# A two-layer graph network in float32 on one core: v's bias moves from a product ahead of the loop into the eviction of the attention output, and the hand-written order of all engines is laid anew

## The chip, the core and the metric

The kernel runs on one core of a Trainium2 chip. The core has five engines with queues of their own: TensorE (PE in the profile; its weight loads are PEld), VectorE (DVE), ScalarE (ACT), GpSimd (POOL) and SyncE (SP), which here only starts transfers. An engine takes its instructions in the order of its queue and waits on semaphores where it needs another engine's result. The metric is the device time of one launch in microseconds. All arithmetic is float32.

## The reference, cut to what matters

128 graphs of 128 nodes with 512 features share one adjacency matrix. Layer 0 is masked attention with eight heads of 64, layer 1 a graph attention whose edge weights come from two row products. Both have a residual and a normalisation.

```python
q = (x @ Wq + bq).reshape(b, n, H, HD)      # k and v likewise
scores = einsum('bqhd,bkhd->bhqk', q, k) / sqrt(HD) + (1 - adj) * -1e9
attn = softmax(scores)
out = einsum('bhqk,bkhd->bqhd', attn, v).reshape(b, n, d) @ Wo + bo
x = layernorm(x + out)
h = x @ W
e = leaky_relu(s1[:, :, None] + s2[:, None, :]) * adj     # s1 = h @ a1, s2 = h @ a2
x = layernorm(x + elu(softmax(e) @ h + beta * h))
```

The rows of `attn` sum to one. A constant bv added to v therefore comes out of the attention as the same constant, and can be added to the attention output in place of v, or, as bv @ Wo, to bo.

## The kernel before

**Tiles and groups.** Two graphs make a group, so there are 64 groups (`NG`), g = 0 to 63; b0 and b1 are the graphs of a group. Five matrix products a group (q, k, v, the output projection w, and h of layer 1) are computed in Strassen-Winograd form: seven block products instead of eight, numbered 1 to 7. `product(name, g, n)` issues one: four matmuls of 128x128 for q and k, two of 128x256 for v, w and h (the profile has two records for each float32 matmul, so eight and four a product). Products 1, 3, 5 and 6 go into the first half of a one-bank PSUM tile, `main[name, g][:, 0]`, product 2 into the second half, `main[..., 1]`, and 7 and 4 into a side tile (`region`). After each of them an engine takes the half out: `take_part` on ScalarE for q, k (two ACTIVATEs that add bq or bk, L347), v and h (a copy, L341), on VectorE for w (L344); `add_block` on VectorE adds a further block to what was taken (L357). The blocks' sums and differences that the right operands need are made by `block_sum` on GpSimd (L252), those of the weights once ahead of the loop by `weight_sum` (L215 to L221).

**One graph through the kernel.** q and k give `scores` (L371), then `mask` and `row_max` (VectorE), `exps` in four pieces of two heads (ScalarE, L393), `row_inv`, `normalise` in four pieces (ScalarE, L407), a write to DRAM and a read back that turn the blocks (`attn_write`, `attn_read`), `turn_attn` (VectorE), `attend` (TensorE, L446: the attention's product with v, into a PSUM tile of 128x512), and `attend_evict`, one ScalarE copy of 128x512 (L455) to `oT`. Product w follows, with the residual that `residual` (GpSimd, L427) made of x and bo. Then come the statistics, the row products, the edge weights (again through DRAM: `weights_write`, `weights_read`, `weights_turn`), `aggregate` (TensorE, L643: the edge weights times the normalised rows), `aggregate_evict` (ScalarE copy of 128x512, L650) to `zT`, product h, ELU (`elu_exp`, `elu_max`, `elu_sum`), `norm_f` (ScalarE, 128x512, L673) and `store`.

**bv before.** `bias_product` (L463) multiplies bv, spread over 128 rows, with Wo, four matmuls of 128x512 into the tile `bop`; `bias_add` (L469) adds it to the spread bo on VectorE. Both run once, ahead of the first residuals.

**The order.** No scheduler sets the order. Each step has a place, a number: `rows(g)` lists the steps of one group, a group is `STEP` = 36.678 further than the one ahead of it, `last_rows(g)` lists the last two groups, `other` holds the places of groups 0 to 3 and NG-4, NG-3, and `at(...)` those of one-time steps. All are sorted by place and issued in that order (L1088), so the places of one engine's steps are its queue. A place of -21 is a step that runs while the group ahead is at +15.7. In the steady part one period holds steps of up to five groups at once. The three queues matter most: TensorE's, ScalarE's with the takes, exps and evictions, and VectorE's. Eight PSUM tiles of one bank (`ps_mm`) serve all products.

In the loop before, the stretch around product q 2 of the next group reads, in places reduced to one period: on TensorE `aggregate b0`, `aggregate b1`, `product q 1`, `w 3`, `w 4`, `h 1`, `h 2`, `k 1`, `q 2`; on ScalarE `exps b1 1`, `aggregate_evict b1`, `exps b1 2`, `exps b1 3`, `take_part q 1`.

Of the kernel before, what the change touches and what calls it, by code (L numbers as in the profile page):

```python
# [8 lines left out]
F32 = mybir.dt.float32  # L9
AF = mybir.ActivationFunctionType  # L10
ALU = mybir.AluOpType
AX = mybir.AxisListType

P = 128
# [8 lines left out]
def gnn_two_layers(  # L23
# [429 lines left out]
    def attend_evict(b):  # L453
        oT[b] = wk2.tile([P, NC, N], F32, tag="oT", name=f"oT_{b}")
        nc.scalar.copy(oT[b], po.pop(b))  # L455


    bop = {}

    def bias_product():  # L460
        bop[0] = ps_mm.tile([P, D], F32, tag="mm", name="bop")
        for c in range(NC):
            nc.tensor.matmul(  # L463
                bop[0], later["bv"][:, c : c + 1].broadcast_to([P, P]), wo_sb[:, c, :],
                start=(c == 0), stop=(c == NC - 1),
            )

    def bias_add():
        nc.vector.tensor_tensor(later["bo"], bop[0], later["bo"], ALU.add)  # L469
# [224 lines left out]
    def rows(g):  # L694

        b0, b1 = g * G, g * G + 1
        return (
            (-39.174, fetch_blocks, g), (-37.005, turn_x, g, 0), (-32.699, turn_x, g, 1),
            (-29.391, block_sum, "x", g, 1), (-29.294, block_sum, "x", g, 3),
            (-27.364, block_sum, "x", g, 2), (-27.09, block_sum, "x", g, 4),  # L700
            (-21.133, product, "q", g, 1), (-20.097, take_part, "q", g, 1, 0, 0),
            (-18.615, fetch_x, b0), (-17.671, product, "k", g, 1), (-16.778, product, "q", g, 2),
            (-16.244, take_part, "k", g, 1, 0, 0), (-14.153, product, "k", g, 2),
            (-13.526, product, "q", g, 6), (-12.548, product, "k", g, 6),
            (-11.443, add_block, "q", g, 2, 0, 0), (-9.494, take_part, "q", g, 6, 1, 0),
            (-9.413, take_part, "k", g, 6, 1, 0), (-8.88, product, "q", g, 7),
            (-7.562, product, "q", g, 5), (-7.442, take_part, "q", g, 5, 1, 1),
            (-7.147, fetch_x, b1), (-6.536, product, "k", g, 5), (-5.906, product, "k", g, 7),
            (-5.896, add_block, "k", g, 2, 0, 0), (-5.725, add_block, "q", g, 7, 1, 1),
            (-5.548, take_part, "k", g, 5, 1, 1), (-5.374, add_block, "k", g, 7, 1, 1),  # L710
            (-5.074, product, "q", g, 3), (-4.492, product, "q", g, 4),
            (-3.636, add_block, "q", g, 4, 1, 0), (-3.595, product, "k", g, 3),
            (-1.748, take_part, "q", g, 3, 0, 1), (-1.398, take_part, "k", g, 3, 0, 1),
            (-0.917, product, "k", g, 4), (-0.78, add_block, "k", g, 4, 1, 0),
            (0.21, residual, b0), (1.068, scores, b0), (1.24, scores, b1), (2.579, mask, b0, 0),
            (3.103, mask, b0, 1), (3.36, product, "v", g, 1), (3.837, row_max, b0),
            (4.328, take_part, "v", g, 1, 0, 0), (5.17, residual, b1), (5.914, exps, b0, 0),
            (6.917, exps, b0, 1), (7.068, mask, b1, 0), (7.248, exps, b0, 2),
            (7.446, product, "v", g, 7), (7.695, product, "v", g, 6), (8.28, exps, b0, 3),
            (8.461, mask, b1, 1), (8.681, product, "v", g, 2), (9.094, row_inv, b0),  # L720
            (9.105, take_part, "v", g, 6, 1, 0), (9.66, add_block, "v", g, 2, 0, 0),
            (9.973, product, "v", g, 5), (10.316, normalise, b0, 0), (10.522, normalise, b0, 1),
            (10.994, normalise, b0, 2), (11.438, row_max, b1), (11.647, normalise, b0, 3),
            (11.961, attn_write, b0), (12.082, exps, b1, 0), (13.41, exps, b1, 1),
            (15.993, exps, b1, 2), (16.038, exps, b1, 3), (16.447, attn_read, b0),
            (17.194, row_inv, b1), (19.051, take_part, "v", g, 5, 1, 1),
            (19.059, normalise, b1, 0), (19.855, normalise, b1, 1), (20.488, normalise, b1, 2),
            (20.957, normalise, b1, 3), (22.331, add_block, "v", g, 7, 1, 1),
            (23.322, attn_write, b1), (27.386, turn_attn, b0, 0), (27.729, attn_read, b1),
            (27.764, turn_attn, b0, 1), (29.975, product, "v", g, 3),  # L730
            (31.059, product, "v", g, 4), (31.551, turn_attn, b1, 0),
            (31.935, add_block, "v", g, 4, 1, 0), (32.067, turn_attn, b1, 1),
            (32.447, take_part, "v", g, 3, 0, 1), (36.678, attend, b0), (37.684, attend, b1),
            (37.775, attend_evict, b1), (39.838, attend_evict, b0),
            (41.008, block_sum, "w", g, 3), (42.314, block_sum, "w", g, 1),
            (42.641, product, "w", g, 1), (42.901, block_sum, "w", g, 2),
            (42.917, product, "w", g, 2), (43.049, take_part, "w", g, 1, 0, 0),
            (43.632, add_block, "w", g, 2, 0, 0), (44.065, block_sum, "w", g, 4),
            (46.147, product, "w", g, 6), (46.327, product, "w", g, 7),
            (47.648, take_part, "w", g, 6, 1, 0), (48.662, product, "w", g, 5),  # L740
            (51.921, take_part, "w", g, 5, 1, 1), (52.41, add_block, "w", g, 7, 1, 1),
            (52.607, product, "w", g, 3), (52.889, product, "w", g, 4),
            (53.077, take_part, "w", g, 3, 0, 1), (53.107, bn_stats, y, b1, "c"),
            (53.43, bn_aggr, b1, "c"), (53.671, add_block, "w", g, 4, 1, 0),
            (54.752, bn_stats, y, b0, "c"), (55.621, bn_aggr, b0, "c"),
            (55.732, add_eps, g, "c"), (57.46, row_product, b1, 0), (57.698, inv_std, g, "c"),
            (57.87, row_product, b0, 0), (58.575, row_product, b0, 1),
            (59.312, row_product, b1, 1), (60.547, scale_s, g), (60.649, s2_turn, g),
            (61.325, norm_c, b1), (61.552, norm_c, b0), (61.886, s2_write, g),
            (64.56, s2_read, g), (70.504, edge, g, 0), (71.072, edge, g, 1), (71.693, leaky, g),  # L750
            (72.789, edge_max, g), (73.852, edge_exp, g), (74.969, edge_inv, g),
            (74.996, weights, g, 0), (75.799, weights, g, 1), (75.843, weights_write, g),
            (83.756, weights_read, g), (84.648, weights_turn, g), (85.676, aggregate, b0),
            (85.957, aggregate_evict, b0), (86.791, aggregate, b1),
            (87.529, aggregate_evict, b1), (88.824, block_sum, "h", g, 1),
            (89.649, block_sum, "h", g, 2), (89.924, product, "h", g, 1),
            (90.085, block_sum, "h", g, 3), (90.326, product, "h", g, 2),
            (92.692, take_part, "h", g, 1, 0, 0), (93.207, block_sum, "h", g, 4),
            (94.908, product, "h", g, 6), (96.85, take_part, "h", g, 6, 1, 0),
            (98.084, product, "h", g, 5), (98.66, take_part, "h", g, 5, 1, 1),  # L760
            (99.044, product, "h", g, 7), (100.674, add_block, "h", g, 7, 1, 1),
            (101.029, product, "h", g, 3), (102.078, product, "h", g, 4),
            (102.268, add_block, "h", g, 2, 0, 0), (102.468, take_part, "h", g, 3, 0, 1),
            (102.705, elu_max, b1), (103.458, add_block, "h", g, 4, 1, 0),
            (105.228, elu_exp, b1), (106.086, elu_max, b0), (108.26, elu_exp, b0),
            (109.53, elu_sum, b1), (114.831, bn_stats, u, b1, "f"), (119.462, bn_aggr, b1, "f"),
            (121.244, elu_sum, b0), (121.784, bn_stats, u, b0, "f"), (123.166, bn_aggr, b0, "f"),
            (123.374, add_eps, g, "f"), (125.473, inv_std, g, "f"), (126.428, shift, g),
            (131.216, norm_f, b1), (134.475, norm_f, b0), (134.599, store, b1),
            (134.901, store, b0),  # L770
        )

    def last_rows(g):

        b0, b1 = g * G, g * G + 1
        if g == NG - 2:
# [133 lines left out]
            (57.237, bn_stats, u, b0, "f"), (57.437, inv_std, g, "f", 1),  # L910
            (57.947, bn_aggr, b0, "f"), (58.127, add_eps, g, "f", 0), (58.457, shift, g, 1),
            (58.477, inv_std, g, "f", 0), (58.807, norm_f, b1), (59.497, shift, g, 0),
            (59.777, store, b1), (59.847, norm_f, b0), (60.817, store, b0),
        )


# [205 lines left out]
```

## Time and profile before

Three runs: median 2389.05 us (2387.67 to 2392.11). The profiled execution took 2389.01 us itself, and its span, first to last instruction, is 2387.2 us.

| what | value |
| --- | --- |
| TensorE clock granted | 0.999 of full |
| busy: TensorE, VectorE, ScalarE, GpSimd | 2364.7, 1943.2, 1529.1, 850.7 us |
| period of the steady loop (from one group's `aggregate` to the next) | 36.59 us |
| `attend_evict`, COPY 128x512, 128 of them | 69.0 us busy, 588 ns each |
| `aggregate_evict`, COPY 128x512, 128 of them | 73.9 us busy, 578 ns each |
| bias ACTIVATE 128x128 of q, 512 of them | 158.3 us busy, 361 ns each |
| `normalise` ACTIVATE 128x128, 1024 of them | 326.1 us busy, 392 ns each |
| `exps` ACTIVATE 128x128, 1024 of them | 398.1 us busy, 391 ns each |

The mean of one instruction is longer than its share of a queue, since instructions behind one another overlap: eight `normalise` ACTIVATEs in a row take 2.45 us, not eight times 0.392. In a line of the timeline the columns are the start, the time of the group of like instructions, the engine, the line of the code and the operation, the written and read names, and the count; in brackets stands how long the engine had been idle before and what released it.

### The profile page before, as it was taken

To read this page: it belongs to the slowest core of one execution; us is meant where nothing else is said; L and a number is where in the kernel's file an instruction comes from. 1 tells how busy PE (TensorE), PEld (TensorE's weight loads), DVE (VectorE), ACT (ScalarE), POOL (GpSimd) and SP (SyncE) were. 2 spreads that over 40 slices of the span, in tenths; PEclk is the share of its full clock that TensorE was granted. 3 is DMA by queue.
4 is the path that set the end of the run, shared out by engine and by line. 5 is a ranking of instruction groups with operands and counts; after the bars stand their busy time and mean duration, and the time that the engine had idled before them with its cause. 6 is when DMAs were issued, how large, how long until landed. Compare 5 with 4: busy or idle time off the path is not lost.

```text
span 2387.2 us, 50256 instructions
## 1 busy us (share of the span) xinstructions
PE 2364.7 (99%) x17716; PEld 2181.7 (91%) x17716; DVE 1943.2 (81%) x4382; ACT 1529.1 (64%) x5376; POOL 850.7 (36%) x1047
## 2 busy tenths in 40 slices
PE   9999999999999999999999999999999999999998
PEld 8998899999999999999999999999999999999986
DVE  6787887887888888878878888788788888887877
ACT  4675666766656666667566666675665666666655
POOL 6242333433423324334333243343343332433332
PEclk9999999999999999999999999999999999999999
DMA  6333434334344343343443433433433434334332
GB/s 191 107 100 108 121 97 125 106 105 133 96 114 123 96 122 114 98 133 96 116 128 94 121 117 101 125 106 105 133 93 117 123 95 124 113 98 133 105 112 75
DMA packets 255900, 269.79 MB, mean 113 GB/s; under 512 B 57424, under 2 KB 204368, under 8 KB 255264
## 3 DMA queue, kind: packets, MB, share of 16 engines
q1 hardware_dynamic: 254704, 265.45, 37.8%
q8 instruction: 140, 2.29, 0.4%
q14 instruction: 112, 0.92, 0.1%
q0 software_dynamic: 400, 0.86, 0.1%
q10 hardware_dynamic: 544, 0.26, 0.0%
HBM read 157.62 MB, written 108.85 MB: 112 GB/s over the span
## 4 chain that ended last, share of the span: by engine, by line
PE 95%; DMA 1%; DVE 1%; ACT 1%; SPq 0%; issue 0%; POOL 0%; ACTq 0%; DVEq 0%
PE pv L293 12%; PE pw L293 11%; PE pq L299 11%; PE pk L299 11%; PE ph L293 11%; PE eq L299 9%; PE psc L371 5%; PE po L446 5%; PE pz L643 5%; PE ew L293 4%; PE eh L293 4%; PE ev L293 4%; DMA wv_sb<-in_L_gnn_Wv_dram 1%; PE plh L328 0%; PE plw L328 0%
## 5 line engine op out<-in xcount | busy, mean ns | idle before, releaser
L393 ACT ACTIVATE s<-s,nmax 128x128 f32<-128x128 f32 x1024 | 398.1, 391 | 87.7 <-DVE nmax L387 87.5
L252 POOL TENSOR_TENSOR tw<-oT 128x256 f32<-128x256 f32 x63 | 51.6, 819 | 1019.6 <-ACT oT L455 1019.6
L407 ACT ACTIVATE sb<-s,rinv 128x128 f32<-128x128 f32 x1024 | 326.1, 392 | 21.1 <-DVE rinv L400 16.2
L341 ACT COPY h<-ph 128x256 f32<-128x256 f32 x252 | 92.9, 369 | 217.2 <-PE ph L293 121.6
L347 ACT ACTIVATE kT<-pk,bk_c 128x128 f32<-128x128 f32 x512 | 160.9, 370 | 103.9 <-DVE kT L357 93.9
L506 DVE SCALAR_TENSOR_TENSOR ya<-w,wa_row 128x512 f32<-128x512 f32 x256 | 220.0, 859 | 4.4
L347 ACT ACTIVATE qT<-pq,bq_c 128x128 f32<-128x128 f32 x512 | 158.3, 361 | 80.1 <-PE pq L299 76.7
L393 ACT ACTIVATION_READ_ACCUMULATOR s<-s,nmax 128x1 f32 x1024 | 192.7, 188 | 0.0
L344 DVE TENSOR_TENSOR w<-pw,x 128x256 f32<-128x256 f32 x252 | 105.8, 420 | 99.2 <-PE pw L293 97.1
L427 POOL TENSOR_TENSOR x<-x,bo_b_in 128x512 f32<-128x512 f32 x128 | 173.2, 1354 | 35.0 <-DMA x<-in_x_dram 33.8
L341 ACT COPY v<-pv 128x256 f32<-128x256 f32 x256 | 94.7, 370 | 132.6 <-PE pv L293 130.4
L436 DVE STREAM_TRANSPOSE attnT<-ab 128x512 f32<-128x512 f32 x256 | 171.7, 691 | 3.1 <-DMA ab<-scr 2.8
L379 DVE SCALAR_TENSOR_TENSOR s<-psc,amask 128x512 f32<-128x512 f32 x256 | 163.4, 678 | 2.9 <-PE psc L371 2.8
L654 ACT ACTIVATE h<-h 128x512 f32<-128x512 f32 x126 | 79.4, 630 | 121.9 <-DVE u L658 121.9
L387 DVE TENSOR_REDUCE nmax<-s 128x8 f32<-128x1024 f32 x128 | 153.2, 1197 | 2.2
L232 DVE STREAM_TRANSPOSE xT<-xblk 128x512 f32<-128x512 f32 x128 | 141.6, 1108 | 7.2 <-DMA xblk<-in_x_dram 7.2
L299 PEld LDWEIGHTS pk<-xT,wk_sb 128*128 128x128 f32 x1024 | 133.7, 192 | 6.9 <-DMA wk_sb<-in_L_gnn_Wk_dram 0.5
L293 PE MATMUL pv<-wv_sb,xT 128*128 128x256 f32 x512 | 137.6, 391 | 0.0
L299 PE MATMUL pq<-xT,wq_sb 128*128 128x128 f32 x1024 | 135.2, 275 | 1.0 <-DMA wq_sb<-in_L_gnn_Wq_dram 1.0
L299 PE MATMUL pk<-xT,wk_sb 128*128 128x128 f32 x1024 | 134.7, 275 | 0.3 <-DMA wk_sb<-in_L_gnn_Wk_dram 0.3
L371 PE MATMUL psc<-kT,qT 64*128 64x128 f32 x2048 | 132.1, 279 | 0.0
L371 PEld LDWEIGHTS psc<-kT,qT 64*128 64x128 f32 x2048 | 119.4, 188 | 11.8 <-issue 11.8
(677 smaller groups left out, 6329.6 us busy)
## 6 DMA issues: line engine op xcount, KB each, us to landing
scr<-sb SPq DMA_DIRECT2D x128, 512.0 KB
ab<-scr SPq DMA_DIRECT2D x512, 128.0 KB
x<-in_x_dram SPq DMA_DIRECT2D x128, 256.0 KB
out_dram<-u SPq DMA_DIRECT2D x128, 256.0 KB
xblk<-in_x_dram SPq DMA_DIRECT2D x254, 128.0 KB
pb<-s2d SPq DMA_DIRECT2D x62, 128.0 KB
attd<-att SPq DMA_DIRECT2D x62, 128.0 KB
ab<-attd SPq DMA_DIRECT2D x248, 32.0 KB
```

Of the source, the lines that this page charges most:

```text
L293: nc.tensor.matmul(out, b[:, c, :], a[:, c, :], start=first and c == 0, stop=(c == 1), skip_group_check=True,)
L299: nc.tensor.matmul(out[:, m * N : (m + 1) * N], a[:, c, m * P : (m + 1) * P], b[:, c, :], start=first and m == 0 and c == 0, stop=(c == 1) ...
L341: nc.scalar.copy(dst, src)
L347: nc.scalar.activation(dst[:, m, :], src[:, m * N : (m + 1) * N], AF.Identity, bias=BIAS[name][:, 2 * i + m : 2 * i + m + 1],)
L371: nc.tensor.matmul(psc[b][j][:, m, :], qT[g][feats, m, rows], kT[g][feats, m, rows], start=True, stop=True,)
L379: nc.vector.scalar_tensor_tensor(s_t[b][:, j * HP : (j + 1) * HP, :], psc[b][j], SCALE, amask.rearrange("p (o n) -> p o n", o=1).broadcast ...
L387: nc.vector.tensor_reduce(nmax[b], s_t[b], AX.X, ALU.max, negate=True)
L393: nc.scalar.activation(s_t[b][:, h, :], s_t[b][:, h, :], AF.Exp, bias=nmax[b][:, h : h + 1], accum_out=rsum[b][:, h : h + 1],)
L407: nc.scalar.mul(sb[b][:, :, h, :], s_t[b][:, h, :].rearrange("p (b c) -> p b c", c=Q), rinv[b][:, h : h + 1],)
L427: nc.gpsimd.tensor_tensor(xr[b], xr[b], later["bo"], ALU.add)
L436: nc.vector.transpose(attnT[b].rearrange("p h (a r) -> p a h r", r=Q)[:, rows], ab[b].rearrange("p a (h c) -> p a h c", c=Q)[:, rows],)
L506: nc.vector.scalar_tensor_tensor(z, y[b], 1.0, wa_row[j], ALU.mult, ALU.mult, accum_out=s12[g][:, i, j : j + 1])
```

## The change

`bias_product` and `bias_add` are gone. `attend_evict` no longer copies the tile of 128x512 at once but takes its four chunks of 128x128 one by one with an ACTIVATE that adds the chunk's column of bv. With it all the places were laid out anew: `rows`, `last_rows`, `other` and the one-time steps.

```diff
     def attend_evict(b):
         oT[b] = wk2.tile([P, NC, N], F32, tag="oT", name=f"oT_{b}")
-        nc.scalar.copy(oT[b], po.pop(b))
-    bop = {}
-    def bias_product():
-        bop[0] = ps_mm.tile([P, D], F32, tag="mm", name="bop")
+        src = po.pop(b)
         for c in range(NC):
-            nc.tensor.matmul(
-                bop[0], later["bv"][:, c : c + 1].broadcast_to([P, P]), wo_sb[:, c, :],
-                start=(c == 0), stop=(c == NC - 1),
-            )
-    def bias_add():
-        nc.vector.tensor_tensor(later["bo"], bop[0], later["bo"], ALU.add)
+            nc.scalar.activation(
+                oT[b][:, c, :], src[:, c, :], AF.Identity, bias=later["bv"][:, c : c + 1]
+            )
...
     def rows(g):
-            (-21.133, product, "q", g, 1), (-20.097, take_part, "q", g, 1, 0, 0),
-            (-18.615, fetch_x, b0), (-17.671, product, "k", g, 1), (-16.778, product, "q", g, 2),
-            (-16.244, take_part, "k", g, 1, 0, 0), (-14.153, product, "k", g, 2),
+            (-24.334, product, "q", g, 1), (-19.387, take_part, "q", g, 1, 0, 0),
+            (-19.354, product, "q", g, 2), (-17.428, product, "k", g, 1),
+            (-14.008, take_part, "k", g, 1, 0, 0), (-13.547, product, "k", g, 2),
...
-            (15.993, exps, b1, 2), (16.038, exps, b1, 3), (16.447, attn_read, b0),
+            (14.154, attn_write, b0), (14.662, exps, b1, 2), (17.142, exps, b1, 3),
...
-            (36.678, attend, b0), (37.684, attend, b1),
-            (37.775, attend_evict, b1), (39.838, attend_evict, b0),
+            (35.106, attend, b0), (35.734, attend, b1), (36.638, attend_evict, b1),
+            (39.369, attend_evict, b0), (39.686, block_sum, "w", g, 1),
...
-            (52.607, product, "w", g, 3), (52.889, product, "w", g, 4),
+            (50.95, product, "w", g, 3), (53.219, product, "w", g, 4),
...
-            (85.676, aggregate, b0), (85.957, aggregate_evict, b0), (86.791, aggregate, b1),
-            (87.529, aggregate_evict, b1), (88.824, block_sum, "h", g, 1),
+            (85.726, aggregate, b0), (88.063, aggregate, b1), (88.6, aggregate_evict, b0),
+            (89.575, aggregate_evict, b1), (89.796, block_sum, "h", g, 1),
...
-    at(27.301, bias_product)
-    at(31.127, bias_add)
```

In places reduced to one period the stretch around product q 2 of the next group now reads, on TensorE: `product q 1`, `aggregate b0`, `w 3`, `aggregate b1`, `w 4`, `q 2`, `h 1`, `h 2`, `k 1`, `h 6`, `h 7`, `k 2`. On ScalarE: `exps b1` 0, 1 and 2, `aggregate_evict b0`, `aggregate_evict b1`, `exps b1 3`, `take_part q 1`, `normalise b1` 0 and 1, `take_part h 1`, `normalise b1` 2 and 3, `norm_f` twice, `take_part k 1`. Among the one-time steps, the loads of x for the first two graphs stand ahead of the blocks of group 1 in SyncE's queue, and the block sums of group 0 ahead of the sums of Wv in GpSimd's.

## The prediction

> **What bounds the kernel now.** I read the busy shares of the page first, then the chain of work that ended last, then the busy time in equal stretches, then TensorE's waits, and last the timelines of TensorE and ScalarE over one period.
>
> ```profile
> PE 2364.7 (99%) x17716; PEld 2181.7 (91%) x17716; DVE 1943.2 (81%) x4382; ACT 1529.1 (64%) x5376; POOL 850.7 (36%) x1047
> ...
> PE 95%; DMA 1%; DVE 1%; ACT 1%; SPq 0%; issue 0%; POOL 0%; ACTq 0%; DVEq 0%
> ```
>
> TensorE is busy for 99% and is 95% of the chain. The stretches (time, length, then the busy time of PE, PEld, DVE, ACT and POOL) show that this is no average over different stages:
>
> ```profile
> 0.00:50.00 50.00, 44.53 (x325) 40.41 (x326) 32.39 (x61) 22.65 (x83) 31.09 (x40) 1.00 0.70 209
> 200.00:300.00 100.00, 96.85 (x696) 88.40 (x695) 78.22 (x182) 64.07 (x230) 35.05 (x44) 1.00 0.39 115
> 300.00:400.00 100.00, 100.00 (x764) 92.78 (x763) 82.93 (x187) 66.25 (x238) 37.36 (x47) 1.00 0.36 103
> ```
>
> From 300 us to 2200 us the same stretches show 0.2 us of idle TensorE in all; it idles 5.5 us at the head, 3.2 us once between 200 and 300, and some 13 us at the end, 9 of them after its last matmul. So work taken from other engines gains nothing, matmuls taken away gain their own length, and any wait that TensorE newly gets in each period is added in full, some sixty times. Its waits now:
>
> ```profile
> PE ph L293 <- POOL th L252: 1.6, 1, 1.6
> PE pq L299 <- ACT qT L347: 1.2, 2, 0.8
> PE eq L299 <- POOL s_v L219: 0.9, 1, 0.9
> ```
>
> (columns: total, times, longest). None recurs with the period. What must be compared is the place where the new order brings a ScalarE result close to the matmul that needs it. In one period, on TensorE and ScalarE:
>
> ```profile
> 1014.51 1.95 PE L643 MATMUL pz<-attT,x 128*128 128x128 f32 x16
> 1016.29 1.06 PE L299 MATMUL pq<-xT,wq_sb 128*128 128x128 f32 x8
> 1017.19 1.03 PE L293 MATMUL pw<-s_w,oT 128*128 128x256 f32 x4
> 1018.05 1.03 PE L293 MATMUL ew<-wo_sb,tw 128*128 128x256 f32 x4
> 1018.92 1.89 PE L293 MATMUL ph<-w_sb,zT 128*128 128x256 f32 x8
> 1020.64 1.05 PE L299 MATMUL pk<-xT,wk_sb 128*128 128x128 f32 x8
> 1021.53 1.06 PE L299 MATMUL pq<-xT,wq_sb 128*128 128x128 f32 x8
> ```
>
> ```profile
> 1016.92 0.57 ACT L650 COPY zT<-pz 128x512 f32<-128x512 f32 x1
> 1017.39 0.40 ACT L393 ACTIVATE s<-s,nmax 128x128 f32<-128x128 f32 x1
> ...
> 1018.94 0.61 ACT L347 ACTIVATE qT<-pq,bq_c 128x128 f32<-128x128 f32 x2
> 1019.44 0.36 ACT L341 COPY v<-pv 128x256 f32<-128x256 f32 x1
> ```
>
> The reader is to see durations (starts are differenced): a q or k product 0.89 us, a v, w or h product 0.866, an aggregate 0.89; on ScalarE the copy of z 0.47 until the next starts, exps of two heads 0.77 (1017.39 to 1018.94 are four heads, 1.55), the take of q 0.61. And a distance: product q 1 starts at 1016.29, its take ends at 1019.55, and product q 2 starts at 1021.53, 2.0 us later.
>
> **What the Trainium skill says.** "PSUM — Partial Sum Buffer", PSUM bank collisions, says that a PSUM bank must be guarded as a bank (by quadrant), not by address: an engine may not read one half while TensorE writes the other. q 1 lies in the first half of its bank and q 2 goes to the second, so q 2 has to wait for the take of q 1; the built program has that wait, on the take's second ACTIVATE, before and after. The trace of before can't show it bite, since 2.0 us lie between. The same page, Engine vs sequencer instructions, says that ScalarE's queue is strictly first in, first out and that matmuls start in program order: nothing can step past the waiting one. The trace agrees as far as it goes: the wait of 0.81 us at 2268.99 on a take of q moved all later matmuls. "ScalarE: Activation LUTs", What ACT_TABLE_LOAD costs, prices an ACTIVATE with a bias column at about 280 ns + 0.833 per element of the row, 93 ns of it overlapped behind another: 0.294 us for 128. The trace has 0.31 (eight `normalise` in 2.45 us) and 0.25 (two takes of q in 0.50 where k follows at once).
>
> **The change part by part.**
>
> *The bias product.* It held TensorE from 33.51 to 36.94, 3.43 us with matmuls on both sides: -3.4. VectorE loses `bias_add`, 0.68 us, and GpSimd two waits on the product (4.56 and 1.24 us); neither was on the path. In GpSimd's queue the block sums of group 0 now stand ahead of the sums of Wv, which takes away the wait of 0.93 above. Against that, x for the first two graphs (2 x 256 KB, about 2.5 us at the 209 GB/s of the first stretch) is now fetched ahead of the blocks of group 1, which may cost up to 2 us. Head: -3, between -5 and -1.
>
> *The eviction.* Eight ACTIVATEs a group in place of two copies: 8 x 0.30 = 2.4 us for 1.07 (the two copies at 1003.90), so +1.3 a group, 64 x 1.3 = 85 us on ScalarE, 1529 to about 1615 of 2387 us, 68%. ScalarE doesn't become the bound. Locally: `attend b1` ends 1.9 us after `attend b0` starts, and product w 1, which reads both results, comes after two scores and v 1 and v 2, 5.6 us after that start. The evictions end at about 2.0 + 2.45 = 4.5. Cover 1.1 us; cost nothing. If an eviction came later by more than that, w 1 would wait for the excess.
>
> *The new order in the loop.* Let E be the end of `aggregate b1`. TensorE's next are w 4 (0.866) and q 2. ScalarE, idle by then, has in its queue: the copy of that aggregate (starts E + 0.11, the hand-off that the profile shows at `attend_evict`; 0.47), exps b1 3 (0.77), the take of q 1 (0.62). Even though q 1 itself had ended 2.6 us before E, its take stands behind a copy that can't begin before E. It ends at E + 0.11 + 0.47 + 0.77 + 0.62 = E + 1.97; the hand-off back to TensorE costs 0.05 to 0.14 (2268.85 to 2268.99 in the wait quoted). q 2 can start at about E + 2.07 and TensorE is ready at E + 0.87: a stall of 1.2 us, known to about 0.1. Behind it stand all of TensorE's matmuls; nobody can make it up, for the engine had no gap. The form holds for groups 3, 4, 5 and 7 to 61, 58 times: 58 x 1.2 = 69.6 us.
>
> *The next hand-off of the same kind.* k 2 waits for the take of k 1. From q 2's start TensorE has 5.24 us of work (q 2, h 1, h 2, k 1, h 6, h 7), so it arrives at E + 7.3. ScalarE after the take of q 1: four ACTIVATEs of `normalise` (1.25, to E + 3.1), the take of h 1 (which ends at E + 3.8; so to E + 4.2), four more (1.2), `norm_f` twice (0.71 each back to back), the take of k 1 (0.62): E + 7.45, and the hand-off: 0.2 late, between 0 and 0.4. 57 x 0.2 = 11.4 us. All other hand-offs of the new order that I followed keep cover: scores behind the last `add_block` of k 0.7 us or more, v 6 and w 6 behind their takes and adds 0.5 or more, `aggregate b0` behind `weights_turn` about 1, the transfers 1.3 or more.
>
> *The transitions.* The first full period was 40.95 instead of 36.59 us (the z copy of graph 7 late, then GpSimd's sum `th`, the 1.6 above). The places of group 3 are new there; I take -2.5, between -4 and +1. The last groups' order has the same kind of chain as before at its end: -1, between -3 and +2.
>
> *Sum*, against the profiled execution's own 2389.01 (its span 2387.2 and 1.8 around it; the median of the runs is 2389.05, the same): 69.6 + 11.4 - 3 - 2.5 - 1 = +74.5, so 2463.5.
>
> **Rivals.** (A) Only q 2 stalls: k 2's 0.2 is within my error, and if ScalarE gains 0.2 us anywhere it is gone: 2389 + 69.6 - 6.5 = 2452. (B) Another hand-off runs out too: ScalarE carries 2.45 us in one block of evictions and VectorE, at 83% in the loop, is followed with 0.5 us of cover in two places. Half a microsecond more for 58 periods is +29: 2492. Against it: a longer period gives VectorE and the transfers more time, not less. (C) The other side, faster: q 2 isn't held by the take, because the halves are guarded apart. Then no stall in the loop and only the gains stay: 2389 - 6.5 = 2382.5. It decides where the stall is under 6.5 / 58 = 0.11 us. For it: no wait of this kind in the trace of before, whose two waits on the take of q are those of q 6 and q 5, which write the same half. Against it: the wait in the built program. (D) Stall small, gains eaten at the head: about 2389, no change.
>
> **How the numbers follow.** Forecast 0.50, A 0.23, B 0.20, C 0.05, D 0.02. The likeliest gives 2463. Its own unknowns: 0.1 x 58 = 6 for the stall, 11 for k 2, 4 for head and transitions: 2446 to 2480. The range reaches down past A and up into B: 2445 to 2486, leaving out C, D and the upper half of B. Differences under 0.2%, 4.8 us, can't be told from no change here. Faster 0.05 (C), same 0.02 (D), slower 0.93.
>
> **What would show it.** A wait of TensorE `pq` on ACT `qT` of about 1.2 us some 58 times, and one of `pk` on `kT` of about 0.2; a period of 37.9 to 38.1 us in place of 36.59; TensorE's share down from 99% to about 96%; ScalarE near 1615 us busy; the row of `bop` gone and no wait on `s_v`. The prediction is wrong if TensorE's stretches stay at 100.00 in the loop, and wrong in its reason if they don't, but wait for something else than the take of q.

## The result and the profile after

The changed kernel took 2612.98 us in the median of four runs (2611.98 to 2616.47), the kernel before 2389.39 beside it: ratio 1.0937, 95% interval 1.0918 to 1.0956. That is 223.6 us more. The direction was forecast, the size was not: 2463 was predicted, with 2486 as the upper end.

The page of the changed kernel, busy shares and the chain that ended last:

```profile
PE 2419.4 (93%) x17708; PEld 2164.7 (83%) x17708; DVE 1919.0 (73%) x4381; ACT 1570.7 (60%) x5760; POOL 845.2 (32%) x1047
...
PE 56%; DVE 25%; ACT 11%; issue 3%; DMA 3%; SPq 1%; DVEq 0%; ACTq 0%
```

TensorE was 95% of the chain and is 56% now. ScalarE has 42 us more to do than before, VectorE 24 less; neither is near the span. The time went into waits. TensorE's, after (total, times, longest):

```profile
PE pq L299 <- ACT qT L347: 63.6, 58, 1.1
PE pk L299 <- ACT kT L347: 56.7, 59, 2.5
PE psc L371 <- DVE kT L357: 27.4, 58, 0.5
PE pv L293 <- DVE v L357: 25.8, 59, 0.5
```

Four waits recur with the period, and the first is the one that was predicted, with its count. The second was predicted at a fifth of its size; the third and fourth (scores on an add of k, v 6 on an add of v) were held to be covered. One period on TensorE:

```profile
1012.54 1.06 PE L299 MATMUL eq<-tx,wq_sb 128*128 128x128 f32 x8
1013.43 1.06 PE L299 MATMUL pk<-xT,s_k 128*128 128x128 f32 x8
...
1017.52 0.72 PE L371 MATMUL psc<-kT,qT 64*128 64x128 f32 x8
1018.75 1.61 PE L371 MATMUL psc<-kT,qT 64*128 64x128 f32 x24 [0.51 <-DVE kT L357]
...
1023.85 1.03 PE L293 MATMUL ev<-s_v,tx 128*128 128x256 f32 x4
1025.31 1.13 PE L293 MATMUL pv<-s_v,tx 128*128 128x256 f32 x4 [0.43 <-DVE v L357]
...
1033.27 1.03 PE L293 MATMUL ew<-wo_sb,tw 128*128 128x256 f32 x4
1035.39 1.16 PE L299 MATMUL pq<-xT,wq_sb 128*128 128x128 f32 x8 [1.10 <-ACT qT L347]
1036.39 1.89 PE L293 MATMUL ph<-w_sb,zT 128*128 128x256 f32 x8
...
1039.88 1.03 PE L293 MATMUL eh<-s_h,th 128*128 128x256 f32 x4
1041.83 1.16 PE L299 MATMUL pk<-xT,wk_sb 128*128 128x128 f32 x8 [0.93 <-ACT kT L347]
```

Difference the starts, don't add the brackets. From w 4 (1033.27) to q 2 (1035.39) are 2.12 us where w 4 alone takes 0.866, and q 2 itself holds TensorE for 1.00 where 0.89 is usual: 1.26 + 0.11 = 1.37 us for a wait listed at 1.10. Likewise k 2 costs 1.09 + 0.11 = 1.2 for 0.93, scores 2.77 to the end of both against 1.98, v 6 0.6 + 0.1. The bracket counts only from the modelled end of the matmul ahead (1033.27 + 1.03 = 1034.30). Without a wait the next product starts 0.866 us after the start of w 4, at 1034.14, so the bracket leaves out about 0.17 us. The period is 40.52 us in place of 36.59: 58 periods of 3.93 us are 228 us, the whole difference and a few us more.

Where the third and the fourth come from is not on TensorE. VectorE in the same period:

```profile
1009.27 0.69 DVE L649 SCALAR_TENSOR_TENSOR u<-h,x 128x512 f32<-128x512 f32 x1
1010.75 0.42 DVE L357 TENSOR_TENSOR qT<-eq,qT 128x256 f32<-128x256 f32 x1 [0.79 <-ACT qT L347]
1014.06 0.42 DVE L357 TENSOR_TENSOR kT<-eq,kT 128x256 f32<-128x256 f32 x1 [2.88 <-PE eq L299]
1014.40 0.41 DVE L357 TENSOR_TENSOR v<-ev,v 128x256 f32<-128x256 f32 x1
...
1018.28 0.41 DVE L357 TENSOR_TENSOR kT<-eq,kT 128x256 f32<-128x256 f32 x1
```

The line at 1014.06 is `add_block k 7`. Product k 7 had run at 1004.6; yet its add waited 2.88 us "for PE eq", until after q 4, which is the first TensorE line above (`eq`, from 1012.54 to 1013.60), had ended. In the whole run this wait is 151.4 us in 61 times, 2.5 us each; in the period shown it is longer than in most. q 7, k 7, q 4 and k 4 share one PSUM bank (the side tile `eq`), and the new order lays this add behind q 4. Everything behind it on VectorE is late with it: the add of v 4, the turns, the edges and the last add of k at 1018.28, on which scores wait; then the masks, `row_max`, the exps, the take and the add of v, on which v 6 waits.

ScalarE shows the same in the chain ahead of k 2:

```profile
1034.73 0.61 ACT L347 ACTIVATE qT<-pq,bq_c 128x128 f32<-128x128 f32 x2
1035.23 1.27 ACT L407 ACTIVATE sb<-s,rinv 128x128 f32<-128x128 f32 x4
1038.32 0.37 ACT L341 COPY h<-ph 128x256 f32<-128x256 f32 x1 [1.82 <-PE ph L293]
1038.59 1.28 ACT L407 ACTIVATE sb<-s,rinv 128x128 f32<-128x128 f32 x4
1039.77 1.50 ACT L664 ACTIVATE u<-u,nmr,rstdf_('f',22)_10204 128x512 f32<-128x512 f32 x2
1041.18 0.60 ACT L347 ACTIVATE kT<-pk,bk_c 128x128 f32<-128x128 f32 x2
```

The take of h 1 (1038.32) starts 0.2 us after h 2 has ended (1036.39 + 1.73 = 1038.12), not after h 1, 0.87 earlier: h 1 and h 2 share a bank, and the take is laid behind h 2. From it the path runs through `normalise` and two `norm_f` to the take of k 1, which ends at 1041.78, and k 2 starts at 1041.83.

### The profile page after: what moved, and what is told of

Read it like the earlier page. It is cut to its first block, busy times and chain, and to the rows that moved or that the text cites. A ratio compares the mean times of both kernels' runs of the same rounds, so it can differ in the third digit from the quotient of the medians.

```text
span 2614.7 us, 50926 instructions
## 1 busy us (share of the span) xinstructions
PE 2419.4 (93%) x17708; PEld 2164.7 (83%) x17708; DVE 1919.0 (73%) x4381; ACT 1570.7 (60%) x5760; POOL 845.2 (32%) x1047
## 4 chain that ended last, share of the span: by engine, by line
PE 56%; DVE 25%; ACT 11%; issue 3%; DMA 3%; SPq 1%; DVEq 0%; ACTq 0%
PE pq L299 11%; PE ph L293 8%; PE pv L293 7%; PE pk L299 7%; PE eq L299 6%; PE pw L293 6%; DVE xT L232 5%; DVE s L379 4%; PE pz L634 4%; ACT sb L407 3%; ACT u L664 3%; DVE attnT L436 3%; DVE nmax L387 3%; DVE att L615 2%; PE ev L293 2%
## 5 line engine op out<-in xcount | busy, mean ns | idle before, releaser
L427 POOL TENSOR_TENSOR x<-x,bo_b_in 128x512 f32<-128x512 f32 x128 | 163.1, 1275 | 855.7 <-DMA x<-in_x_dram 827.2
L407 ACT ACTIVATE sb<-s,rinv 128x128 f32<-128x128 f32 x1024 | 319.8, 391 | 21.5 <-DVE rinv L400 20.6
L299 PEld LDWEIGHTS pq<-xT,wq_sb 128*128 128x128 f32 x1024 | 129.4, 191 | 92.2 <-ACT qT L347 86.9
L299 PE MATMUL pq<-xT,wq_sb 128*128 128x128 f32 x1024 | 140.9, 281 | 65.3 <-ACT qT L347 63.6
L299 PE MATMUL pk<-xT,wk_sb 128*128 128x128 f32 x1024 | 142.0, 282 | 56.8 <-ACT kT L347 56.4
L497 DVE SCALAR_TENSOR_TENSOR ya<-w,wa_row 128x512 f32<-128x512 f32 x256 | 174.7, 682 | 2.3
L252 POOL TENSOR_TENSOR tw<-oT,oT 128x256 f32<-128x256 f32 x63 | 48.6, 771 | 390.7 <-ACT oT L458 374.1
L371 PE MATMUL psc<-kT,qT 64*128 64x128 f32 x2048 | 148.1, 285 | 27.5 <-DVE kT L357 27.4
L357 DVE TENSOR_TENSOR kT<-eq,kT 128x256 f32<-128x256 f32 x128 | 53.6, 418 | 151.4 <-PE eq L299 151.4
L458 ACT ACTIVATE oT<-po,bv_c 128x128 f32<-128x128 f32 x512 | 137.7, 372 | 6.4 <-PE po L446 6.3
```

The costliest lines, as they stand in the source:

```text
L299: nc.tensor.matmul(out[:, m * N : (m + 1) * N], a[:, c, m * P : (m + 1) * P], b[:, c, :], start=first and m == 0 and c == 0, stop=(c == 1) ...
L371: nc.tensor.matmul(psc[b][j][:, m, :], qT[g][feats, m, rows], kT[g][feats, m, rows], start=True, stop=True,)
L407: nc.scalar.mul(sb[b][:, :, h, :], s_t[b][:, h, :].rearrange("p (b c) -> p b c", c=Q), rinv[b][:, h : h + 1],)
L427: nc.gpsimd.tensor_tensor(xr[b], xr[b], later["bo"], ALU.add)
L497: nc.vector.scalar_tensor_tensor(z, y[b], 1.0, wa_row[j], ALU.mult, ALU.mult, accum_out=s12[g][:, i, j : j + 1])
```

## The experiments

All times are medians; "less" is against the 2612.98 of the changed kernel.

| run | edit | us | against the kernel before |
| --- | --- | --- | --- |
| x_kadd | changed kernel, add of k 7 laid ahead of q 4 | 2528.86 | 1.0578 (1.0559 to 1.0598) |
| x_qtake | changed kernel, take of q 1 earlier on ScalarE | 2536.14 | 1.0609 (1.0589 to 1.0628) |
| x_ktake | changed kernel, take of k 1 ahead of `norm_f` | 2546.28 | 1.0651 (1.0632 to 1.0671) |
| x_all | all three | 2381.90 | 0.9966 (0.9952 to 0.9979) |
| x_q2order | changed kernel, q 2 laid ahead of the take of q 1 | 2537.37 | 1.0611 (1.0592 to 1.0630) |
| x_h2 | changed kernel, h 2 laid behind the take of h 1 | 2566.04 | 1.0731 (1.0711 to 1.0750) |
| x_copy | changed kernel, eviction in one copy | 2625.62 | 1.0980 (1.0960 to 1.1000) |
| b_evict | kernel before, eviction in four pieces, no bias product | 2393.53 | 1.0014 (1.0007 to 1.0021) |
| b_quiet | b_evict with GpSimd quiet at the head | 2389.24 | 0.9992 (0.9984 to 1.0000) |
| x_all2 | x_all, and k 2 later in groups 6 and 7 | 2378.91 | 0.9948 (0.9934 to 0.9962) |

### The third and fourth wait: x_kadd

```diff
-            (-5.177, product, "q", g, 4), (-5.022, add_block, "k", g, 7, 1, 1),
+            (-5.177, product, "q", g, 4), (-5.2, add_block, "k", g, 7, 1, 1),
```

The list is sorted by place, so -5.2 is issued ahead of -5.177.

> The changed kernel with one place altered: add_block k 7 at -5.2 instead of -5.022, so that it stands ahead of product q 4 (-5.177) and not behind it. Every engine's queue holds the same instructions in the same order as in the changed kernel; only the waits differ. Theory (bank order): add_block k 7 waited for q 4, because both use the one bank of the side tile and it was laid behind it; that wait of 2.9 us on VectorE delays the adds ahead of scores and the masks. With it gone TensorE's waits 'psc on DVE kT' (27.4 us) and 'pv on DVE v' (25.8 us) vanish, the period falls from 40.5 to about 38.8 us, and the time to 2505 to 2530 us. Rival (VectorE or the four-piece eviction is simply too long for the new order): both waits stay, time within 15 us of 2613.

It took 2528.86 us, 84.1 less, and both waits are gone from TensorE's list. VectorE in this run:

```profile
1017.22 0.43 DVE L357 TENSOR_TENSOR qT<-eq,qT 128x256 f32<-128x256 f32 x1 [0.79 <-ACT qT L347]
1018.11 0.42 DVE L357 TENSOR_TENSOR kT<-eq,kT 128x256 f32<-128x256 f32 x1 [0.47 <-ACT kT L347]
1018.46 0.41 DVE L357 TENSOR_TENSOR v<-ev,v 128x256 f32<-128x256 f32 x1
```

The add of k 7 now follows the add of q 7 after 0.89 us, where it was 3.31, and waits only for the take of k 5 that it adds to. Since no queue changed, neither VectorE's load nor the eviction can be the cause; the order of two steps of different engines in one bank is. (The side tile fills its bank, so the runs don't tell whether the wait goes by the tile or by the bank.)

### The first wait: x_qtake and x_q2order

Two ways to take it away. The first moves the take on ScalarE:

```diff
-            (-24.334, product, "q", g, 1), (-19.387, take_part, "q", g, 1, 0, 0),
+            (-24.334, product, "q", g, 1), (-20.47, take_part, "q", g, 1, 0, 0),
```

> The changed kernel with take_part q 1 at -20.47 instead of -19.387, so that in ScalarE's queue it stands ahead of aggregate_evict b1 and exps b1 3. Theory: the wait 'pq on ACT qT' (63.6 us, 58 times) goes and with it some 0.27 us of restart each, so 58 x 1.37 = 79 us less: 2525 to 2545 us, the other three waits staying as they are. Rival (ScalarE as a whole is late, the wait only moves): another wait grows by as much, 'pk on ACT kT' above all, and the time stays above 2580.

2536.14 us, 76.8 less (1.32 a period), and the other three waits stayed: 56.9, 27.5 and 25.8 us. The second leaves all queues as they are and turns the order within the bank round:

```diff
-            (-19.354, product, "q", g, 2), (-17.428, product, "k", g, 1),
+            (-19.4, product, "q", g, 2), (-17.428, product, "k", g, 1),
```

> The changed kernel with product q 2 at -19.4 instead of -19.354, so that it is laid ahead of take_part q 1 (-19.387). Every engine's queue keeps its instructions and their order; only who waits for whom in this bank is turned round. Theory: q 2 no longer waits ('pq on ACT qT' gone, 1.37 us a period), but the take of q 1 now waits for q 2 and ends 0.6 us later, which makes the wait of k 2 about 0.2 to 0.4 us longer than the 0.93 now: 2540 to 2560 us. Rival (the wait is on the take's data, not on the order in the bank): no change, 2613 us.

2537.37 us, 75.6 less. The wait on the take of q is gone here too, and that of k 2 grew only from 56.7 to 58.3 us in all, so that the time lies below the range that I had given. So q 2 needs nothing that the take makes; it waits because it is laid behind it in one bank.

### The second wait: x_ktake and x_h2

```diff
-            (-14.008, take_part, "k", g, 1, 0, 0), (-13.547, product, "k", g, 2),
+            (-15.0, take_part, "k", g, 1, 0, 0), (-13.547, product, "k", g, 2),
```

> The changed kernel with take_part k 1 at -15.0 instead of -14.008, so that in ScalarE's queue it stands ahead of the two norm_f. Theory: 'pk on ACT kT' (56.7 us, 59 times) goes with its restart, 58 x 1.2 = 70 us less: 2535 to 2555 us, the other waits staying. Rival (the take of k 1 is late because take_part h 1, which waits for product h 2, is late, and norm_f plays no part): at most half of it goes, above 2580.

2546.28 us, 66.7 less; the wait on the take of k fell from 56.7 to 3.2 us in three places.

```diff
-            (90.935, product, "h", g, 1), (91.475, product, "h", g, 2),
+            (90.935, product, "h", g, 1), (93.0, product, "h", g, 2),
```

> The changed kernel with product h 2 at 93.0 instead of 91.475, behind take_part h 1 (92.995) in the order, and behind product k 1 in TensorE's queue. Theory: take_part h 1 waited for h 2, since both use one bank and it was laid behind h 2; now it waits for h 1 alone and comes 0.9 us or more earlier, so that the take of k 1 comes earlier: 'pk on ACT kT' falls from 56.7 to 10 to 25 us, the time to 2560 to 2585 us. Rival (the take of k 1 is late through normalise and norm_f alone): the wait stays within 10 us of 56.7.

2566.04 us, 46.9 less; the listed wait fell to 3.8 us, further than the 10 to 25 expected. Here `norm_f` stands where it stood, and only the take of h 1 comes earlier: 2.06 us after the start of q 2 (1016.18 to 1018.24) in place of 2.93. Both links of the chain are real, and either of them gives most of it back: the 0.87 us for h 2, and the 1.4 us of `norm_f` ahead of the take of k 1. That x_h2 gains 20 us less than x_ktake is what is left of k 2's delay without a bracket: from the product ahead of it to k 2 are 1.10 us there (1020.66 to 1021.76) instead of 0.866, and k 2 takes 0.1 longer, 0.34 us in 58 periods.

### The sum: x_all and x_all2

> The three edits together (take_part q 1 at -20.47, take_part k 1 at -15.0, add_block k 7 at -5.2). Theory: all four recurring waits go, the period comes back to 36.6 us and the time to 2380 to 2392 us, about the kernel before or a few us below it. Rival (the waits hide others of the same size, the new order has no cover left): 2420 us or more.

2381.90 us: 231.1 less, against 227.7 for the three single gains. None of the recurring waits is left, and the timeline's stretch is full:

```profile
PE 2354.6 (99%) x17708; PEld 2175.1 (91%) x17708; DVE 1933.8 (81%) x4381; ACT 1589.5 (67%) x5760; POOL 848.0 (36%) x1047
...
1000.00:1100.00 100.00, 100.00 (x734) 92.73 (x731) 80.95 (x187) 69.44 (x253) 37.43 (x47) 1.00 0.36 114
```

(the page's busy shares, and one of the stretches as shown before). The period is 36.50 us. With three numbers altered, the change is 0.34% faster than the kernel before. What TensorE still waited for in x_all were, among others, two takes of k in the transitions of groups 6 and 7, so k 2 was moved there:

```diff
+            if g in (6, 7) and fn is product and args[0] == "k" and args[2] == 2:
+                place = -11.0
```

> The three edits together, and for groups 6 and 7 alone product k 2 at -11.0, behind k 7. Theory: the waits of 1.8 and 1.1 us for the take of k 1 in these two transitions go with 0.27 us of restart each: 3.4 us less than with the three edits, 2377 to 2380 us. Rival (they move on to the next take): within 1 us of 2382.

2378.91 us, 3.0 less than x_all; of the waits for a take of k one of 0.4 us is left. This is the fastest version: 0.52% below the kernel before.

### Is it the eviction? x_copy

```diff
-        src = po.pop(b)
-        for c in range(NC):
-            nc.scalar.activation(
-                oT[b][:, c, :], src[:, c, :], AF.Identity, bias=later["bv"][:, c : c + 1]
-            )
+        nc.scalar.copy(oT[b], po.pop(b))
```

> The changed kernel with its new order, but attend_evict is one copy of 128x512 again; v's bias is left out of the computation. Theory: the four recurring waits of TensorE don't come from the eviction, so all four stay and the time is 2605 to 2618 us. Rival (ScalarE is made late by the four-piece eviction): the waits shrink, 2580 us or less.

2625.62 us, 12.6 more, outside what either theory said. Three waits are the same to 0.1 us; that of v 6 rose from 25.8 to 36.8. So the eviction isn't what made the change slow, but giving it back makes it slower. `weights` on VectorE (att) is what grew: first the changed kernel, then x_copy (count, busy, mean ns):

```profile
L615 DVE SCALAR_TENSOR_TENSOR att<-ee,einv,beta_i 128x128 f32<-128x128 f32 x128 | 66.7, 562 | 2.2
```

```profile
L611 DVE SCALAR_TENSOR_TENSOR att<-ee,einv,beta_i 128x128 f32<-128x128 f32 x128 | 77.0, 639 | 2.2
```

With oT ready earlier, GpSimd begins its sums for product w earlier, beside `weights`, and these ahead of the masks take 10.3 us more in the run, about what the run lost. In x_all they take 349 ns each; in the period looked at, VectorE is through with them (at 1036.8) before GpSimd starts (at 1037.55). That this is the cause of the 12.6 us is read from the traces, not tested by a run.

### The words of the change alone: b_evict and b_quiet

```diff
-        nc.scalar.copy(oT[b], po.pop(b))
+        src = po.pop(b)
+        for c in range(NC):
+            nc.scalar.activation(
+                oT[b][:, c, :], src[:, c, :], AF.Identity, bias=later["bv"][:, c : c + 1]
+            )
...
-    at(27.301, bias_product)
-    at(31.127, bias_add)
```

> The kernel before with its own order, and of the change only the part in words: attend_evict in four ACTIVATEs with v's bias, no bias_product, no bias_add. Theory: the eviction is hidden and the product's 3.4 us are gained, 2383 to 2388 us, no recurring wait of TensorE. Rival (the eviction costs in the loop): a recurring wait of product w on ACT oT or of exps, 2400 us or more.

2393.53 us: 0.14% slower, not 3 us faster. The period is 36.59 us as before, so the eviction in four pieces is hidden, as expected. Much of the loss is at the head: TensorE waits 1.84 and 2.66 us there for takes of k, which stand behind `normalise` and `row_inv`. VectorE in this run, and then GpSimd:

```profile
35.80 1.45 DVE L179 SCALAR_TENSOR_TENSOR wa_t<-w_sb,uf_in 128x512 f32<-128x512 f32 x1
...
37.30 1.66 DVE L179 SCALAR_TENSOR_TENSOR wa_t<-w_sb,uf_in 128x512 f32<-128x512 f32 x1
...
39.01 1.66 DVE L179 SCALAR_TENSOR_TENSOR wa_t<-w_sb,uf_in 128x512 f32<-128x512 f32 x1
...
40.60 0.19 DVE L400 RECIPROCAL rinv<-rsum 128x8 f32<-128x8 f32 x1
```

```profile
33.76 2.95 POOL L427 TENSOR_TENSOR x<-x,bo_b_in 128x512 f32<-128x512 f32 x2
36.67 1.74 POOL L219 TENSOR_TENSOR s_w<-wo_sb 128x512 f32<-128x512 f32 x1
```

In the kernel before the three columns ahead of `row_inv` took 0.68 to 0.69 us. VectorE, and then GpSimd:

```profile
32.99 0.68 DVE L179 SCALAR_TENSOR_TENSOR wa_t<-w_sb,uf_in 128x512 f32<-128x512 f32 x1
...
33.71 0.69 DVE L179 SCALAR_TENSOR_TENSOR wa_t<-w_sb,uf_in 128x512 f32<-128x512 f32 x1
...
34.45 0.69 DVE L179 SCALAR_TENSOR_TENSOR wa_t<-w_sb,uf_in 128x512 f32<-128x512 f32 x1
```

```profile
35.54 1.46 POOL L217 TENSOR_TENSOR wo_sb<-wo_sb 128x512 f32<-128x512 f32 x1 [4.56 <-PE bop L463]
```

GpSimd stood still from 31.0 to 35.5, waiting for the bias product; once it ran again, a column at 35.91 took 1.63 us there too. That wait looked free to remove; it had kept GpSimd out of VectorE's way ahead of `row_inv`. The test makes GpSimd quiet there:

```diff
-        nc.gpsimd.tensor_tensor(xr[b], xr[b], later["bo"], ALU.add)
+        if b > 3:
+            nc.gpsimd.tensor_tensor(xr[b], xr[b], later["bo"], ALU.add)
...
-    at(31.127, weight_sum, "w", 1, nc.gpsimd)
```

> The kernel before with its own order, four-piece eviction and no bias product, and with GpSimd made quiet between 32 and 37 us: the sum w 1 of Wo and the residual's addition of bo for graphs 0 to 3 are left out of the computation. Theory: in the run without the bias product GpSimd no longer waited for it, ran beside VectorE's wa_column and stretched these from 0.69 to 1.66 us, which delayed row_inv, normalise and the takes of k (TensorE waits of 1.84 and 2.66 us). With GpSimd quiet the columns behind 36 us take 0.7 us, the wait of 2.66 goes, and the time is 2386 to 2391 us. Rival (the head is late for another reason, the blocks of x that land late): the waits on kT stay and the time is 2392 us or more.

```profile
33.92 1.60 DVE L179 SCALAR_TENSOR_TENSOR wa_t<-w_sb,uf_in 128x512 f32<-128x512 f32 x1
...
35.57 0.69 DVE L179 SCALAR_TENSOR_TENSOR wa_t<-w_sb,uf_in 128x512 f32<-128x512 f32 x1
...
36.30 0.69 DVE L179 SCALAR_TENSOR_TENSOR wa_t<-w_sb,uf_in 128x512 f32<-128x512 f32 x1
...
36.92 0.20 DVE L400 RECIPROCAL rinv<-rsum 128x8 f32<-128x8 f32 x1
```

2389.24 us in 13 runs, 4.3 less than b_evict in 21. The column that still runs beside GpSimd's sums (they end at 35.0) takes 1.60 us, those behind it 0.69, and `row_inv` comes 3.7 us earlier. Not all of this is the edit's: in the profiled execution of b_evict the head was 2.1 us later already ahead of these columns. Most of that is TensorE's clock. First b_evict, then b_quiet:

```profile
25.36 1.70 PE L299 MATMUL eq<-tx,wq_sb 128*128 128x128 f32 x8 [2.45 <-DVE kT L357]
26.85 1.91 PE L299 MATMUL eq<-tx,wk_sb 128*128 128x128 f32 x8
```

```profile
24.91 1.13 PE L299 MATMUL eq<-tx,wq_sb 128*128 128x128 f32 x8 [1.41 <-DVE kT L357]
25.88 1.06 PE L299 MATMUL eq<-tx,wk_sb 128*128 128x128 f32 x8
```

Between 26 and 28 us the granted clock was 0.50 in b_evict and 1.00 in b_quiet, and from the first of these products to `scores` passed 4.46 us against 2.82. A like dip lies at 224 to 226 us of b_evict alone. What the edit did in the head is the other 1.6 us: TensorE's wait of 2.66 us fell to 1.08, where I had expected it to go; the one of 1.84 stayed.

The clock is a second cause in the medians too. Its mean over the runs was 0.9976 in b_evict, 0.9985 in the kernel before beside it and 0.9987 in b_quiet. Taking only runs with a mean clock of 0.998, the medians are 2393.37, 2391.38 and 2389.71: a loss of 2.0 us and not 2.8, of which b_quiet gives 3.7 back and not 4.3. So the collision is shown, and that it is part of b_evict's loss; why the clock was lower in b_evict, and what sets the wait of 1.84, which lies where the bias product stood before, was not tried.

## Why the prediction was right in direction and wrong in size

**Right: the first wait.** Its place, its cause, its count of 58 and its price held: 69.6 us were forecast, taking it away gave 76.8 (x_qtake). Most of the difference (58 x 0.11 = 6.4 us) is the 0.11 us by which the first product behind a wait is slower, which the sum had left out.

**The gains: the sum near, the parts not.** The rest of the change was put at -6.5 us. x_all, which has the change without the recurring waits, is 8.5 below the kernel before (2381.90 against 2390.41). The parts are not as forecast, so that the sum comes near is in part luck. In the old order, taking the bias product away and evicting in four pieces is not worth 3.4 us but loses 2.8 (b_evict), in part because the sum priced the wait that GpSimd loses at nothing. In x_all 57 periods give 0.09 us each (36.50 against 36.59), some 5 of the 8.5 us; this wasn't foreseen, and no run says where it comes from.

**Right: the eviction is hidden.** Eight ACTIVATEs take 2.14 us in the loop (2.4 forecast); b_evict has the old period. The load was put too high: the four-piece evictions are busy for 137.7 us where the copies took 69.0, 69 more and not 85, and ScalarE as a whole reached 1570.7 us in place of the 1615 forecast.

**Wrong: the second wait, a term mis-sized.** "The take of h 1 (which ends at E + 3.8; so to E + 4.2)" took the end of h 1 as the point from which its take may run. In the changed kernel it runs from the end of h 2, 0.87 us later. The stall was 1.2 us instead of 0.2 (x_ktake gave 66.7 us back where 11.4 had been put), and x_h2 shows the 0.87 as the larger part of the difference.

**Wrong: the step "all other hand-offs of the new order that I followed keep cover: scores behind the last `add_block` of k 0.7 us or more, v 6 and w 6 behind their takes and adds 0.5 or more".** The prediction gives no working for these covers, and those of scores and of v 6 did not hold. They would have held for a chain on VectorE that starts from the end of v 4, as in x_kadd. In the changed kernel it starts from the end of q 4, since the add of k 7, which stands ahead of the add of v 4 in VectorE's queue, is laid behind q 4 in one bank. Against the next `attend` (`po` at 1015.62; 1021.79 in x_kadd) the add of v 4 came 1.22 us ahead of it and 3.33 in x_kadd, 2.1 us late. The sum had put nothing here, and it was 84.1 us. Of the 149 us between forecast and result this step is 84, and the second wait 55. The rival B had the right shape, a further hand-off that runs out, but no place, and its half a microsecond was a fifth of what came: 3.93 us a period were lost in all, and 1.4 were forecast.

**One cause for both.** The prediction cited the Trainium skill, "PSUM — Partial Sum Buffer", PSUM bank collisions, for one direction: a product waits for a take that is laid ahead of it in its bank. The page's rule names any two engines, so it has a second: a take or an add is kept apart from the products too, and in this kernel it waits for the products laid ahead of it in its bank, whichever half they write (the add of k 7, in one half, waited for q 4, in the other). The third and fourth wait come from the second direction, through one add. In the second wait k 2 waits by the first direction, for a take that is late by the second. The kernel before showed neither as a loss: there the take of h 1 is laid behind h 2 too, but had slack, and the add of k 7 stands ahead of q 4 (-5.374 against -4.492). The places of the changed kernel did show it, and I followed the first direction only. x_kadd and x_q2order, in which no queue changes, show both directions apart.

The band of the likeliest case was too narrow by its own terms as well: 2446 to 2480 is 17 us to each side, the 6 and the 11 without the 4 for head and transitions.

## What to carry to other kernels

Where steps of several engines share a PSUM bank, as here, the order in which they are laid matters as much as the order in each queue: in this kernel two steps on different engines that don't need each other's data waited for one another when they touched the same one-bank tile, and swapping their places, which changed no queue, took 84.1 us away in one case and 75.6 in another. So list for each eviction the last product laid ahead of it in its tile, not only the one it reads. Where one engine is full, price a new recurring wait from the starts on both sides of it, about 0.27 us above what the list of waits says here, and look at what a removed wait had been keeping apart.

## What the runs showed of the hardware

A VectorE instruction with two inputs from SBUF took up to 2.4 times as long beside GpSimd's sums. `wa_column` took 0.69 us alone and mostly 1.45 to 1.66 beside them, though only 0.87 in one case (b_evict, at 33.47). `weights` took 349 ns in x_all, and in the mean 562 and 639 where GpSimd's sums ran beside a part of them. The Trainium skill, "SBUF — State Buffer", Who interferes with whom, states that such an instruction contends with GpSimd's reads; the runs agree and give the size here. By this reading an earlier GpSimd made b_evict slower, in part, as b_quiet shows; that an earlier eviction made x_copy slower in the same way is not shown by a run of its own.
